# Sixteen-sequence attention and expert block on one core: the last sequence's output projections split into eight parts, its residual, norm and gates moved behind the first expert list

## The chip, the cores and the metric

The kernel runs on one core of a Trainium2 chip. The metric is the device time of one launch in microseconds (us), taken as the median of three runs. A core has a matrix engine (TensorE, PE in the tables), a vector engine (VectorE, DVE), an activation engine (ScalarE, ACT), a general engine (GpSimd, POOL) and a queue that issues transfers (SyncE, SP). Each engine runs its own instructions strictly in the order in which the kernel was built, and the engines wait for one another by semaphores.

## The reference

The input is x of 16 sequences, 256 tokens and 256 features. What matters here, cut from the reference:

```python
h = _ln(x, ln1_g, ln1_b) + shift
qkv = (h @ Wqkv.T).reshape(b, n, 3, H, HD)          # 16 heads of 64
...                                                 # norms of q and k, softmax attention
x = x + o @ Wout.T                                  # output projection and residual
tok = x.reshape(-1, d)                              # 4096 tokens
gate = jax.nn.softmax(tok @ Wgate.T, axis=-1)       # 8 experts
k_cap = bs // E                                     # 512
vals, idx = jax.lax.top_k(gate.T, k_cap)            # each expert takes its 512 best tokens
g = _ln(tok[idx_flat], mlp_g, mlp_b)
y = gelu(g @ fc1[e].T + b1) @ fc2[e].T + b2         # per expert, weighted by the gate
tok = tok.at[idx_flat].add(y.reshape(-1, d))
```

## The kernel before

**Attention.** Each of the 16 sequences is two tiles of 128 tokens. The steps of all sequences are laid into one list (`plan.step`, in the code `at`), and each step has a number in the table `PLACES`. The steps are emitted in the order of these numbers, so `PLACES` alone sets the order of instructions on every engine. The numbers are places and not times of the profile.

**The tail of a sequence** (class `Tail`, once for each of its two tiles): `project` (L936) is the output projection, eight matmuls with 256 columns each, which the profile counts as 16 because the data is float32; `residual` (L943, then the statistics L623 and L625) runs on DVE; `power` (L629, L106) on POOL; `apply` (L635) on DVE writes the normed tokens; `transposes` (L962) on PE, `evict` (L968) on ACT, `gate` (L973) on PE and `gate_evict` (L979) on DVE make the gate logits; `store` (L947) and `store_norm` (L957) go through SP.

**The search.** The first routing picks, for every expert, tokens out of the first 15 sequences (half of the capacity), so it needs nothing from the last one. It finds the threshold of each expert bit by bit, in 30 rounds. In a round DVE compares (`compare_less`, L1101), PE counts with one small matmul into `pc` (`count_over`, L1110), and DVE decides the bit (`decide`, L1125). A round cannot begin before the one ahead is decided. The last sequence's attention is spread between these rounds on the other engines. Behind the counts of the last 20 rounds stand four transposes of an identity matrix on PE (`fill`, L557), which compute nothing that is used.

**The lists.** After the search come masks, running sums and places (L1140 to L1183). Then each of 16 jobs (8 experts of the first routing, 8 of the second) gets its list: `onehot` (L1246) makes 30 tiles on DVE, `list_matmul` (L1254) puts them through PE into `pls`, `take` (L1263, L1265) reads the row numbers and weights, and `gather` (L1270) fetches the rows by two indirect DMAs that POOL issues. `transposes` (L1279) into `px` and `evict` (L1286) bring the rows into the layout for `up` (L1333), `gelu` and `down` (L1353). On PE the order around the first job is: list 0, fillers (`fill(16)` twice), 20 of the 30 matmuls of list 1, `px` of job 0, 5 more of list 1, `fill(8)`, the last 5, and then `up` of job 0. The second routing, which does need the last sequence, begins inside job 1.

**PSUM.** `ps` has three tags that matter: `mm` with 3 buffers, `sc` with 4 and `po` with one. The gate logits `pl` and the list sums `pls` share the single buffer of `po`.

Of the kernel before, what the change touches and what calls it, by code (L numbers as in the profile page):

```python
# [9 lines left out]
F32 = mybir.dt.float32  # L10
# [8 lines left out]
P = 128  # L19
B, N, D = 16, 256, 256  # L20
# [8 lines left out]
HP = H // 2  # L29
# [37 lines left out]
def kernel(  # L67
# [84 lines left out]
    def make_others():  # L152
# [352 lines left out]
        742.67, 743.91, 745.19, 752.11, 757.25, 758.03, 744.67, 746.15, 753.02, 754.08, 757.05,  # L505
        749.01, 758.75, 759.99, 745.47, 746.71, 747.5, 753.93, 763.49, 764.15, 747.31, 748.46,
        755.75, 756.81, 757.54, 749.78, 765.16, 747.51, 749.18, 752.52, 754.84, 755.9, 756.56,
        749.95, 751.07, 756.66, 764.69, 765.35, 753.76, 766.36, 767.6, 772.57, 776.44, 777.59,
        777.59, 778.45, 778.96, 779.57, 780.01, 780.87, 781.59, 776.07, 779.94, 781.09, 781.09,
        781.95, 782.46, 781.32, 781.76, 782.25, 782.93, 224.23, 226.04, 227.04, 228.04, 229.04,  # L510
        230.04, 731.12, 732.47, 733.9, 750.61, 745.77, 747.11, 747.91, 749.11, 749.55, 750.55,
        751.06, 751.82, 751.51, 752.17, 752.42, 753.17, 752.87, 753.52, 753.93, 754.52, 754.38,
        754.72, 754.97, 755.57, 755.42, 755.92, 756.17, 756.72, 756.62, 756.92, 757.18, 757.72,
        757.63, 757.93, 758.18, 758.72, 758.63, 758.93, 759.18, 759.77, 759.63, 760.12, 760.38,
        760.92, 760.83, 761.13, 761.38, 761.92, 761.83, 762.13, 762.38, 762.93, 762.83, 763.13,
        763.13, 763.59, 764.13, 763.39, 764.33, 764.33, 764.58, 765.13, 765.03, 765.33, 769.09,
        765.59, 766.18, 766.04, 766.53, 768.09, 766.78, 767.38, 767.23, 767.73, 767.73, 767.98,
        768.53, 768.43, 768.73, 768.73, 768.99, 769.53, 769.44, 769.74, 769.73, 769.99, 770.53,
        770.44, 770.74, 770.74, 770.99, 771.54, 771.44, 771.74, 771.74, 772, 772.54, 772.45,
        772.75, 780.15, 773, 776.04, 773.45, 776.24, 780.51, 777.44, 779.54, 777.89, 779.74,  # L520
        779.79, 780.94, 781.54, 781.39, 781.75, 781.74, 782.28, 782.83, 782.73, 783.09, 783.03,
        783.34, 783.89, 783.79, 784.09, 784.09, 784.35, 784.89, 784.8, 785.1, 785.09, 785.35,
        785.89, 785.8, 786.1, 786.1, 786.35, 786.9, 786.8, 787.1, 787.1, 787.36, 787.9, 787.81,
        788.11, 788.1, 788.36, 788.9, 788.81, 789.11, 789.1, 789.36, 790.58, 790.58, 792.03,
        793.25, 794.37, 790.9, 794.37, 806.29, 753.97, 751.5, 767.6, 795.32, 795.32, 796.32,
        796.94, 797.85, 795.32, 798.92, 796.13, 799.28, 798.56, 799.64, 797.75, 800, 800.36,
        800.78, 800.36, 802.18, 805.94, 805.28, 805.94, 800.78, 801.43, 803.78, 802.24, 804.14,
        803.05, 804.5, 803.86, 804.86, 804.67, 805.72, 805.48, 806.84, 809.23, 809.65, 814.15,
        814.84, 808.23, 809.55, 812.55, 815.55, 807.18, 808.27, 808.05, 809.14, 808.92, 810.01,
        811.53, 812.62, 810.66, 811.75, 813.27, 814.36, 809.79, 810.88, 812.4, 813.49, 807.43,  # L530
        814.94, 818.62, 818.4, 822.08, 819.22,
    )

    if True:
# [5 lines left out]
        ps = ctx.enter_context(tc.tile_pool(name="ps", bufs=1, space=PSUM))  # L540
# [387 lines left out]
        class Tail:  # L928
# [2 lines left out]

            def project(self, a=0, b=HP):
                if a == 0:
                    self.pw = ps.tile([P, D], F32, tag="mm", bufs=3, name="pw")
                for hp in range(a, b):
                    nc.tensor.matmul(  # L936
                        self.pw, oTs[self.b][:, hp // 2, self.t, hp % 2, :], wo[:, hp, :],
                        start=(hp == 0), stop=(hp == HP - 1),
                    )
# [260 lines left out]
        class Job:  # L1200
# [177 lines left out]
            mm=3, sc=4, po=1, xs=5, hT=2, qT=2, kT=2, v=2, oT=2, xn=4, sq=2, ss=4, qk=3, nmax=8,  # L1378
            sums=4, pr=PRB, pb=3, qraw=2, prT=4, blocks=4, tok=3, tn=2, tokT=2, pa=1, l1=4, l2=4,
        ))  # L1380
        at = plan.step
# [19 lines left out]
        for b in range(B):  # L1401
# [6 lines left out]
            a = First(b)  # L1408
# [9 lines left out]
            for (g, t), p in GROUP.items():  # L1418
                p += base
                a = Group(b, g, t)  # L1420
                n = (b, g, t)
# [27 lines left out]
            for d in range(HP // 2):  # L1449
                a = Quad(b, d)  # L1450
                p = base + d * QUAD
                g = d // 2
                n = (b, d)
                po = ("po", 0) + n
# [24 lines left out]
            for t in range(TB):  # L1479
                a = Tail(b, t)  # L1480
                p = base + TAIL[t]
                n = (b, t)
                pw, tok, tn, tokT, l2, pg, pl = ("mm", 4) + n, ("tok",) + n, ("tn",) + n, ("tokT",) + n, ("l2",) + n, ("mm", 5) + n, ("po", 1) + n
                at(p, "PE", 3.47, a.project, [("oT", b)], [pw], [pw, ("oT", b)], lag=0.22)
                at(p + 4, "DVE", 1.0, a.residual, [pw], [tok], [pw, ("xs", b), tok, l2], lag=0.15)
                at(p + 5, "SP", 0.5, a.store, [tok], (), [tok], lag=2.0)
                at(p + 5, "POOL", 0.76, a.power, [tok], [l2], [l2])
                at(p + 6, "DVE", 0.33, a.apply, [l2], [tn], [l2, tok, tn], lag=0.18)
                at(p + 7, "SP", 0.5, a.store_norm, [tn], [("xnd", b)], [tn], lag=2.0)
                at(p + 6, "PE", 0.22, a.transposes, [tok], [pg], [tok, pg], lag=0.22)  # L1490
                at(p + 7, "ACT", 0.3, a.evict, [pg], [tokT], [pg, tokT], lag=0.19)
                at(p + 8, "PE", 0.45, a.gate, [tokT], [pl], [tokT, pl], lag=0.22)
                at(p + 9, "DVE", 0.16, a.gate_evict, [pl], [("gates", b)], [pl])
# [21 lines left out]
        for n in range(29, -1, -1):  # L1515
            pc = ("mm", 99, 30 - n)
            at(top + 1.3 * (30 - n), "DVE", 0.45, partial(first.compare_less, n), [("cand", n + 1)], [("cnt", n)], lag=0.095)
            at(top + 1.3 * (30 - n) + 0.1, "PE", 0.03, partial(first.count_over, n), [("cnt", n)], [("pc", n)], [pc], lag=0.17)
            at(top + 1.3 * (30 - n) + 0.2, "DVE", 0.2, partial(first.either, n), [("cand", n + 1)], [("next", n)])
            at(top + 1.3 * (30 - n) + 0.3, "DVE", 0.2, partial(first.decide, n), [("pc", n), ("next", n)], [("cand", n)], [pc], lag=0.053)  # L1520
            if n < 20:
                at(top + 1.3 * (30 - n) + 0.2, "PE", 0.36, partial(fill, 4), [("pc", n)], (), [("sc", 98, n)], lag=0.22)
        p1, p2 = ("mm", 99, 31), ("mm", 99, 32)
        top += 50
# [13 lines left out]
        for n in range(2):  # L1538
            a = jobs[n]
# [5 lines left out]
            for i in range(6):  # L1545
                name, took, by = {"D": ("DVE", 0.81, nc.vector), "P": ("POOL", 1.4, nc.gpsimd), "A": ("ACT", 3.5, nc.scalar)}[who[i]]
# [54 lines left out]
        for k in range(1, len(jobs)):  # L1601
            a = jobs[k]
# [4 lines left out]
            for s in range(SLOTS):  # L1607
# [36 lines left out]
                else:  # L1644
                    i, q = divmod(s - FC, 4)
# [66 lines left out]
```

## Time and profile before

| what | value |
|---|---|
| median of three runs | 1072.86 us (1072.36 to 1073.65) |
| the profiled execution, own time | 1076.07 us |
| its span in the trace | 1074.4 us |
| mean granted TensorE clock | 0.987 |
| busy: PE, DVE, ACT, POOL | 1039.2, 825.8, 588.7, 615.8 us |
| first list's row numbers ready on DVE (L1263) | begins at 814.03 us |
| first `up` matmul (L1333) | begins at 821.19 us |

Times of the trace count from the start of the span. A busy share is the time in which at least one instruction of the engine ran. The granted clock is the share of full speed that TensorE was allowed in a stretch. "Idle before" and the arrow in square brackets name the time an engine stood still before an instruction and what ended it.

### The profile page before, as it was taken

The page shows a single profiled execution, that of the slowest core. Times are in us where ns is not written, and L with a number is a line of the kernel's source. Part 1 is how long each engine was busy: PE and PEld are TensorE (multiplying, and loading weights), DVE is VectorE, ACT ScalarE, POOL GpSimd, SP SyncE. Part 2 cuts the span into 40 slices and gives each one's busy share as a digit, 9 for nine tenths or more (in the row PEclk, how much of TensorE's full clock was granted, in tenths as well). Part 3 has the DMA queues.
Part 4 walks back from the last instruction along what each step waited for, and adds up shares of the span by engine and source line. Part 5 has one row for each costly group of instructions (what it writes and reads, how often), then busy time and mean ns, then how long its engine had stood idle before and what let it go on. Part 6 is the DMA issues. An engine that isn't in the chain of part 4 may idle for free. (4 is left out here: it accounts for less than half of the span.)

```text
span 1074.4 us, 17749 instructions
## 1 busy us (share of the span) xinstructions
PE 1039.2 (97%) x5519; PEld 680.7 (63%) x5519; DVE 825.8 (77%) x2295; ACT 588.7 (55%) x1646; POOL 615.8 (57%) x997
## 2 busy tenths in 40 slices
PE   7899999999999999999999999999789999999996
PEld 4455656555554655656565565666568888888885
DVE  6667888989887898798888888888667588656530
ACT  1577676676666666575766667675503422332331
POOL 3666776778667686666767676674401433333332
PEclk9999999999999999999999999999899999999998
DMA  6014889888887898887888888888530656667772
GB/s 217 1 59 157 270 292 325 291 291 280 305 275 264 284 317 309 289 287 271 286 295 301 285 299 286 289 314 288 176 103 21 195 143 182 197 199 202 219 233 30
DMA packets 169710, 250.53 MB, mean 233 GB/s; under 512 B 9744, under 2 KB 139536, under 8 KB 169616
## 3 DMA queue, kind: packets, MB, share of 16 engines
q1 hardware_dynamic: 161696, 239.11, 65.5%
q0 software_dynamic: 6144, 8.39, 4.3%
q10 hardware_dynamic: 1776, 1.90, 0.5%
q8 instruction: 44, 0.72, 0.3%
q14 instruction: 50, 0.41, 0.1%
HBM read 142.67 MB, written 106.69 MB: 232 GB/s over the span
## 5 line engine op out<-in xcount | busy, mean ns | idle before, releaser
L696 PE MATMUL pm<-wq,hT 128*128 128x512 f32 x768 | 360.8, 607 | 7.9 <-DVE qk L733 4.2
L843 ACT ACTIVATE pr<-sc,nmax 128x256 f32<-128x256 f32 x512 | 237.3, 479 | 102.4 <-DVE nmax L830 86.7
L854 POOL TENSOR_SCALAR pr<-pr,sums 128x256 f32<-128x256 f32 x512 | 237.0, 481 | 97.6 <-DVE sums L850 91.6
L696 PEld LDWEIGHTS pm<-wq,hT 128*128 128x128 f32 x768 | 137.8, 191 | 162.9 <-issue 136.2
L106 POOL TENSOR_TENSOR ss<-ss,neghalf 128x8 f32<-128x8 f32 x128 | 210.5, 1645 | 10.6
L830 DVE TENSOR_REDUCE nmax<-sc 128x2 f32<-128x512 f32 x256 | 165.7, 676 | 15.1 <-PE sc L822 14.4
L864 DVE STREAM_TRANSPOSE pb<-pr 128x512 f32<-128x512 f32 x232 | 153.9, 686 | 7.2 <-POOL pr L854 6.7
L822 PE MATMUL sc<-kT,qT 64*128 64x256 f32 x1024 | 135.2, 394 | 0.0
L910 PE MATMUL po<-prT,v 128*64 128x256 f32 x1024 | 128.8, 389 | 0.0
L709 ACT ACTIVATE sq<-pm 128x512 f32<-128x512 f32 x128 | 76.7, 604 | 92.4 <-PE pm L696 91.4
L1370 POOL DMA_INDIRECT out<-y,idx x32 | 50.9, 1591 | 124.7 <-DVE oh L1246 59.9
L822 PEld LDWEIGHTS sc<-kT,qT 64*128 64x128 f32 x1024 | 91.3, 186 | 46.9 <-issue 28.5
L1333 PE MATMUL ph<-xT,w 128*128 128x256 f32 x512 | 116.9, 383 | 2.2 <-ACT xT L1318 2.2
L936 PE MATMUL pw<-wo,oT 128*128 128x256 f32 x512 | 115.2, 381 | 0.0
L1353 PE MATMUL py<-w,hid 128*128 128x256 f32 x512 | 115.1, 380 | 0.0
L936 PEld LDWEIGHTS pw<-wo,oT 128*128 128x128 f32 x512 | 96.3, 190 | 21.0 <-issue 6.0
L910 PEld LDWEIGHTS po<-prT,v 128*64 128x64 f32 x1024 | 66.7, 137 | 65.3 <-issue 19.6
L843 ACT ACTIVATION_READ_ACCUMULATOR pr<-sc,nmax 128x1 f32 x512 | 108.0, 211 | 0.0
L733 DVE TENSOR_TENSOR qk<-pm,ss 128x512 f32<-128x512 f32 x128 | 89.7, 702 | 22.1 <-POOL ss L106 20.0
L1333 PEld LDWEIGHTS ph<-xT,w 128*128 128x128 f32 x512 | 95.0, 190 | 16.4 <-ACT xT L1318 3.5
L1353 PEld LDWEIGHTS py<-w,hid 128*128 128x128 f32 x512 | 96.1, 190 | 13.2
L713 DVE TENSOR_REDUCE ss<-sq 128x8 f32<-128x512 f32 x128 | 85.0, 669 | 22.8 <-ACT sq L709 21.3
(144 smaller groups left out, 1058.3 us busy)
## 6 DMA issues: line engine op xcount, KB each, us to landing
blocks<-pb SPq DMA_DIRECT2D x116, 512.0 KB
prT<-blocks SPq DMA_DIRECT2D x116, 512.0 KB
kblocks<-kb SPq DMA_DIRECT2D x60, 512.0 KB
w<-in_fc2T SPq DMA_DIRECT2D x16, 1024.0 KB
qraw<-kblocks SPq DMA_DIRECT2D x30, 512.0 KB
kT<-kblocks SPq DMA_DIRECT2D x30, 512.0 KB
w<-in_fc1T SPq DMA_DIRECT2D x9, 1024.0 KB
w<-in_fc1Q SPq DMA_DIRECT2D x7, 1024.0 KB
```

Source lines behind the costliest of these rows:

```text
L106: nc.gpsimd.tensor_tensor(dst, src, neghalf[:, : src.shape[1]], ALU.pow)
L696: nc.tensor.matmul(self.pm, hTs[self.b][:, c, bass.ts(self.t, P)], wq[:, c, bass.ts(self.g, GW)], start=(c == 0), stop=(c == DC - 1),)
L733: engine.tensor_tensor(dst, src.rearrange("p (q e d) -> p q e d", q=QB, e=8), by_head(self.ss[:, 1, :]), ALU.mult,)
L822: nc.tensor.matmul(self.sc[i, j][:, t, :], qTs[self.b][rows, hp, bass.ts(t, P)], keys[rows, hp] if whole else keys[rows, hp // 4, hp % 4], ...
L830: nc.vector.tensor_reduce(self.nmax[i, j], self.sc[i, j], AX.X, ALU.max, negate=True)
L843: nc.scalar.activation(dst, src, AF.Exp, bias=self.nmax[i, j][:, t : t + 1], scale=1.0, accum_out=self.sums[i][:, 0, j, t : t + 1],)
L854: nc.gpsimd.tensor_scalar(self.pr[i, j][:, t, :], self.pr[i, j][:, t, :], self.sums[i][:, 1, j, t : t + 1], 1.0, ALU.mult, ALU.mult,)
L864: nc.vector.transpose(self.pb[i][:, :, :, j].rearrange("p k c t n -> p t k c n"), self.pr[i, j].rearrange("p t (k c m) -> p t k c m", c=TB ...
L910: nc.tensor.matmul(self.po[j * HD : (j + 1) * HD, i, :], vs[self.b][:, c, bass.ts(4 * self.d + 2 * i + j, HD)], prT[:, j, c] if (self.b, s ...
L936: nc.tensor.matmul(self.pw, oTs[self.b][:, hp // 2, self.t, hp % 2, :], wo[:, hp, :], start=(hp == 0), stop=(hp == HP - 1),)
L1333: nc.tensor.matmul(self.ph[f], self.w1[:, c, bass.ts(f, P)], self.xT[:, :, c].rearrange("p k i n -> p k (i n)") if self.exchanged else sel ...
L1353: nc.tensor.matmul(self.py[i], self.hid[:, f, bass.ts(i, P)], self.w2[:, f, :], start=(f == 0), stop=(f == FC - 1),)
```

## The change

The two projections of the last sequence, which stood whole behind two counts of the search, are cut into four parts of two matmuls (four in the profile's count) each. One part stands behind each of eight counts, and the four filler transposes that stood behind these counts are left out. The target of these projections moves from the PSUM tag `mm` to `sc`. All that follows them (residual, power, apply, transposes, evict, gate, gate_evict, both stores) gets places behind `take` of the first list; the projections of the other 15 sequences are untouched. Seen on the engines: on DVE both residuals with their statistics stand between `take` of list 0 and `gives` of list 1, and both `apply` and both `gate_evict` between that and the 30 one-hot tiles of list 1; on POOL both `power` stand between the two gathers of job 0 and those of job 1; on PE the gate's transposes and matmuls stand between the two `fill(16)`; on SP the second job's weights are issued ahead of the four stores, as before.

```diff
     PLACES = (
...
-        749.95, 751.07, 756.66, 764.69, 765.35, 753.76, 766.36, 767.6, 772.57, 776.44, 777.59,
-        777.59, 778.45, 778.96, 779.57, 780.01, 780.87, 781.59, 776.07, 779.94, 781.09, 781.09,
-        781.95, 782.46, 781.32, 781.76, 782.25, 782.93, 224.23, 226.04, 227.04, 228.04, 229.04,
+        749.95, 751.07, 756.66, 764.69, 765.35, 753.76, 766.36, 767.6, 769.54, 770.54, 771.55,
+        772.55, 800.37, 800.83, 800.79, 800.82, 800.85, 800.82, 800.84, 800.89, 800.91, 776.05,
+        779.55, 781.55, 782.84, 800.38, 800.84, 800.8, 800.83, 800.86, 800.83, 800.85, 800.95,
+        800.97, 224.23, 226.04, 227.04, 228.04, 229.04, 230.04, 731.12, 732.47, 733.9, 750.61,
...
             def project(self, a=0, b=HP):
                 if a == 0:
-                    self.pw = ps.tile([P, D], F32, tag="mm", bufs=3, name="pw")
+                    tag, bufs = ("sc", 4) if self.b == B - 1 else ("mm", 3)
+                    self.pw = ps.tile([P, D], F32, tag=tag, bufs=bufs, name="pw")
...
-                at(p, "PE", 3.47, a.project, [("oT", b)], [pw], [pw, ("oT", b)], lag=0.22)
+                steps = 4 if b == B - 1 else 1
+                for i in range(steps):
+                    part = (i * HP // steps, (i + 1) * HP // steps)
+                    at(p, "PE", 3.47 / steps, (partial(a.project, *part) if steps > 1 else a.project), [("oT", b)] + ([(1, pw, i)] if i else []), [(1, pw, i + 1)] + ([pw] if i == steps - 1 else []), [pw, ("oT", b)], lag=0.22)
...
-            if n < 20:
+            if n < 20 and not 5 < n < 14:
                 at(top + 1.3 * (30 - n) + 0.2, "PE", 0.36, partial(fill, 4), [("pc", n)], (), [("sc", 98, n)], lag=0.22)
```

## The prediction

> **What bounds the kernel now.** I read the page first: PE is busy for 1039.2 of 1074.4 us, so what counts is whether PE's order stands still, and where. The timeline of PE through the search shows the rounds that the change touches:
>
> ```profile
> 785.25 0.16 PE L1110 MATMUL pc<-cnt,twice 128*128 128x1 bf16 x1 [0.34 <-DVE reach L1101]
> 785.28 0.64 PE L557 MATMUL fill<-ident 128*128 128x128 f32 x4
> 786.25 0.16 PE L1110 MATMUL pc<-cnt,twice 128*128 128x1 bf16 x1 [0.34 <-DVE reach L1101]
> ...
> 787.28 3.70 PE L936 MATMUL pw<-wo,oT 128*128 128x256 f32 x16
> 790.82 0.17 PE L1110 MATMUL pc<-cnt,twice 128*128 128x1 bf16 x1
> 790.84 3.70 PE L936 MATMUL pw<-wo,oT 128*128 128x256 f32 x16
> 794.38 0.17 PE L1110 MATMUL pc<-cnt,twice 128*128 128x1 bf16 x1
> ...
> 798.82 0.16 PE L1110 MATMUL pc<-cnt,twice 128*128 128x1 bf16 x1 [0.34 <-DVE reach L1101]
> ```
>
> A plain round lasts 1.00 us and waits for DVE's compare (PE idles 0.34). Where a whole projection stands between two counts, the count comes 3.54 us after the projection began and nothing is idle on PE: there PE holds the search. Next, the same view where the first list hands over to the first job (DVE, POOL and PE, one after the other):
>
> ```profile
> 814.03 0.16 DVE L1263 TENSOR_REDUCE idx<-pls 128x2 int32<-128x4 f32 x1 [0.40 <-PE pls L1254]
> 816.06 0.96 POOL L1270 DMA_INDIRECT xg<-xn_dram,idx  x1 [0.30 <-issue]
> 819.55 0.64 PE L1279 MATMUL px<-ident,xg 128*128 128x128 f32 x4
> 820.02 0.27 PE L1254 MATMUL pls<-give,oh 128*128 128x10 bf16 x5
> 820.15 1.07 PE L557 MATMUL fill<-ident 128*128 128x128 f32 x8
> 821.06 0.27 PE L1254 MATMUL pls<-give,oh 128*128 128x10 bf16 x5
> 821.19 7.15 PE L1333 MATMUL ph<-xT,w 128*128 128x256 f32 x32
> ```
>
> The first job starts behind the whole of list 1 in PE's order, so whatever makes DVE late with list 1's one-hot tiles makes the first `up` late. After 821.19 PE has no gap for the next jobs (in the stretches from 821 to 870 its busy time equals their length), so a shift of the first `up` carries over to the end. Last, the busy time cut into stretches of 3.41 us, with the granted clock in the third column from the end:
>
> ```profile
> 801.30:804.71 3.41, 2.18 (x17) 1.48 (x16) 2.91 (x18) 0.00 (x0) 0.00 (x0) 1.00 0.82 289
> 811.53:814.95 3.42, 3.04 (x35) 2.34 (x35) 2.98 (x19) 0.96 (x4) 0.45 (x1) 1.00 0.02 7
> 814.95:818.36 3.41, 3.41 (x18) 3.41 (x17) 3.41 (x23) 0.00 (x0) 1.77 (x2) 0.50 0.27 77
> ```
>
> The clock was halved at 814.95 and came back at 818.36, although PE counts as busy for 3.04 us of the stretch ahead. What differs is the work: list matmuls of 10 columns, with only about 1.1 us of transposes, against 2.18 us of fillers that kept it.
>
> **What is saved: the search.** From the count at 784.25 to the one at 798.82 are eight rounds in 14.57 us. A projection of 16 took 3.54, so a part of 4 takes 0.885 us; with the 0.03 from count to first matmul that is 0.92, under the 1.00 of the round that DVE sets (a round with eight filler transposes, about 0.97 from 783.28 to the next count, also held 1.00). DVE's residuals (1.01 each, from 791.19 to 792.20), `apply` and gate copies leave these rounds too. Eight rounds at 1.00 make 8.00: the search ends **6.57 us** earlier. The removed fillers cost nothing to take out, since the parts keep PE denser than they did. The move to the `sc` tag leaves two buffers for the fillers of rounds 5 to 0; one filler group per round needs no more. Job 1's weights wait for the last projection (SP's issue at 794.61) and now go out about 2 us earlier, into a quiet DMA stretch; the row gather comes later, so I count nothing.
>
> **What is given back: list 1.** I count from the start of the first list's row numbers (0 = 814.03 before), at full clock.
> - DVE: both residuals stand ahead of list 1's `gives`: 2 x 1.01, so `gives` moves from 0.15 to 2.17 and ends its slot at 2.69.
> - POOL: both `power` are queued behind the two gather issues, which end at 2.99. With the 0.30 that POOL showed after one such issue (the trace has no arithmetic behind one; between 0 and 0.30, I take 0.30, the only row) the first `power` ends at 4.11 (0.82, from 792.37 to 793.19), the second at 4.93. DVE's two `apply` wait for them, the second until about 4.97, and behind them wait the gate copies and all 30 one-hot tiles.
> - One buffer: the second gate matmul needs the `po` buffer that the first gate copy frees. Copy 5.29 to 5.46, matmul at 5.51, second copy 0.55 to 0.65 later (795.97 to 796.52, 797.27 to 797.92), first one-hot 0.10 after it, at 6.21. Before: 0.67 (814.70). **5.54 us later.**
> - PE: `px` waits for 20 one-hots and the last fillers for 25. The tiles come at 0.167 each (30 in 5.00), 25 by 10.38; from the five list matmuls at 820.02 to `up` were 1.17, of which 0.1 is the first of them, so `up` starts at about 11.5 instead of 7.16: **4.34 us** back.
>
> The rows themselves are no limit: those of job 0 were there by 819.55 (5.5), now `px` comes at 9.6. Those of job 1: its row numbers come 7.09 after its first one-hot (814.70 to 821.79), at 13.3; the DMA activity ended 3.8 after them (825.6), at 17.1; PE gets there 6.99 after `up` starts, at 18.5. The four stores wait on SP behind the new `apply`; behind them stands only job 2's load, which waits for job 0's `down` anyway. Second routing and later one-hots begin with job 1 and have 5.33 us of DVE idle ahead of them before (832.27).
>
> **The clock.** At full clock the sum is 6.57 - 4.34 = 2.23 us saved. But PE now waits in pieces: between list 0 and `up` it has 11.5 us, and in them two groups of 16 fillers (1.75 each), the gate's transposes (0.5), `px` (0.5) and eight fillers (0.9). From the end of the second group at 7.8 to `up` at 11.5 only 1.4 us of dense work lies in 3.7 us. The rows bracket the limit: 1.1 in 3.41 lost the clock, about 1.5 (three filler rounds, 0.5 each without pipeline end) kept it. If it is lost there, `px` and eight fillers take up to 1.4 more and the first 3.41 us of `up` do half their work, 1.7 more: 0 to 3.1; less than 0 is excluded, for the 2.23 has no half clock on its path. Between the ends I take 1.4, because 1.4 lies nearer to the row that kept the clock and the stretches need not fall on the worst place. The sum is **0.8 us saved**: 1076.07 becomes 1075.2 for the profiled execution, which ran 3.2 above the median (its clock and times are those of one run); the same step on the median gives 1072.0.
>
> [...]
>
> **The rivals.**
> 1. *No clock lost* (faster): 2.23 saved, up to 3.0 if POOL has no gap behind its issues and the waits are a little shorter: 1070.6 (1069.8 to 1070.7). For it: the 1.4 against 1.5 is close. Against it: the halved clock at 814.95 in the same kind of work.
> 2. *Half clock all along* (slower): the clock drops at list 0 as before, the thin stretch behind it (gate matmuls of 8 columns, waits) cannot bring it back, as 774.00 to 777.42 with 1.88 us busy stayed at 0.50, and it stays halved through `px`, the fillers and two stretches of `up`: 1.4 + 3.4 = 4.8 lost, 2.6 slower, 1075.4. It decides for the slower side from 2.23 + 2.15 = 4.4 us of loss on.
> 3. *A part does not fit in a round*: the round with attention matmuls from 781.12 to 782.24 took 1.12. Eight such rounds cost 1.0 of the gain: 1071.6 to 1073.0, with or without the clock; it stays in the middle case.
>
> **How the numbers follow.** A measurement of this kernel tells about 0.2% from no change, 2.15 us. The middle case (0.8 saved, between 2.15 saved and 2.15 lost) has 0.45, rival 1 has 0.30, rival 2 has 0.25. The middle case alone spans 1070.8 to 1075.0. The range 1069.8 to 1075.6 takes in the best of rival 1 and the price of rival 2, and leaves out what lies beyond either. The time is that of the middle case.
>
> **What would show it.** In the profile after: counts 1.00 apart with four `pw` matmuls between them from the count at 784.25 on; row numbers of list 0 near 807.5; then 5.5 us until list 1's first one-hot, with DVE's `apply` ended by POOL's `power`; `up` 11.5 behind the row numbers, near 819.0 at full clock and 820 to 821 with the loss; and a clock of 0.50 in a stretch between. Wrong would be: counts wider than 1.1 apart, a one-hot start much before 5 us, or a gap at job 1's `px`.

## The result, and the profile after

The changed kernel took 1071.01 us (median of 20 runs), the kernel before, measured beside it, 1073.37 (20 runs). The ratio is 0.9978, with a 95% interval of 0.9969 to 0.9987: **2.4 us saved, between 1.4 and 3.3**. The profiled execution took 1070.36 us (span 1068.6). Lines of the new kernel from L936 on are one higher than before.

PE's timeline through the search, with start, duration and, in brackets, the idle time ahead:

```profile
782.44 0.16 PE L1111 MATMUL pc<-cnt,twice 128*128 128x1 bf16 x1
782.47 1.11 PE L937 MATMUL pw<-wo,oT 128*128 128x256 f32 x4
783.44 0.16 PE L1111 MATMUL pc<-cnt,twice 128*128 128x1 bf16 x1
...
790.47 0.16 PE L1111 MATMUL pc<-cnt,twice 128*128 128x1 bf16 x1
```

The same eight rounds that took 14.57 us (784.25 to 798.82) now take 8.03 (782.44 to 790.47). The bracket is gone: PE waits for nothing ahead of a count, and the round is still 1.00. The hand-over from list 0 to the first job, in the timelines of DVE, POOL and PE:

```profile
805.74 0.16 DVE L1264 TENSOR_REDUCE idx<-pls 128x2 int32<-128x4 f32 x1 [0.42 <-PE pls L1255]
809.69 0.41 DVE L635 TENSOR_SCALAR tn<-tok,mv,rs 128x256 f32<-128x256 f32 x1 [1.17 <-POOL rs L106]
810.61 0.41 DVE L635 TENSOR_SCALAR tn<-tok,mv,rs 128x256 f32<-128x256 f32 x1 [0.50 <-POOL rs L106]
811.86 0.17 DVE L980 COPY gates<-pl 128x8 f32<-128x8 f32 x1 [0.77 <-PE pl L974]
811.94 4.97 DVE L1247 TENSOR_SCALAR oh<-lane,partf 128x128 bf16<-128x128 bf16 x30
807.77 0.96 POOL L1271 DMA_INDIRECT xg<-xn_dram,idx  x1 [0.31 <-issue]
808.80 0.19 POOL L629 TENSOR_SCALAR rs<-mv 128x1 f32<-128x1 f32 x1
811.24 0.58 PE L974 MATMUL pl<-wg,tokT 128*128 128x8 f32 x4 [0.95 <-DVE gates L980]
817.23 7.15 PE L1334 MATMUL ph<-xT,w 128*128 128x256 f32 x32
```

Both `apply` wait for POOL, the second gate matmul for the first gate copy (the one `po` buffer), the second copy for that matmul. List 1's first one-hot tile starts at 811.94, 6.20 us behind the row numbers, and `up` 11.49 behind them; before it was 0.67 and 7.16. Last, the busy time in stretches of 3.41 us (PE first, the granted clock third from the end):

```profile
805.22:808.63 3.41, 3.41 (x23) 3.35 (x23) 2.72 (x11) 0.00 (x0) 2.12 (x2) 0.50 0.23 55
808.63:812.04 3.41, 2.21 (x19) 1.91 (x18) 1.08 (x5) 0.65 (x2) 1.61 (x5) 1.00 0.45 151
812.04:815.45 3.41, 3.41 (x36) 3.35 (x35) 3.41 (x22) 0.00 (x0) 0.00 (x0) 0.50 0.07 24
815.45:818.86 3.41, 3.41 (x33) 3.14 (x31) 3.31 (x16) 1.49 (x3) 0.00 (x0) 1.00 0.03 7
```

The clock drops twice: over the first 16 fillers (0.50 from 805.22), where it dropped in the kernel before too (0.50 from 814.95), and again between the lists (0.50 from 812.04), as the prediction feared. But the 16 fillers of the second group fill that second slow stretch, and `up` begins 1.78 us after full speed is back. In this run the second drop cost nothing.

### One table for all runs

Medians of the kernel before went from 1071.85 to 1073.28 us over four chips, so the traces are read by four intervals on one path. *Search*: from the count behind which the first part stands (784.25 before, the same count in all) to the first matmul of the totals (804.84 before). *List 0*: to the first list's row numbers. *List 1*: to the first `up`. *Job 0*: to the `up` of job 1 (835.53 before). Sum is their change against 51.28; time is ratio minus one, times the median of before on the same chip, with the interval.

| run | search | list 0 | list 1 | job 0 | sum | time, us |
|---|---|---|---|---|---|---|
| before | 20.59 | 9.19 | 7.16 | 14.34 | | |
| before, second trace | 20.58 | 9.19 | 7.16 | 14.33 | 0.0 | +0.1 (-1.4 to 1.5) |
| after | 14.02 | 9.28 | 11.49 | 14.33 | -2.2 | -2.4 (-3.3 to -1.4) |
| after, second trace | 14.02 | 9.26 | 12.64 | 14.83 | -0.5 | -1.8 (-3.3 to -0.2) |
| parts only, tail in the search | 17.33 | 9.19 | 7.15 | 14.34 | -3.3 | -2.9 (-4.1 to -1.8) |
| tail moved only, no parts | 19.53 | 9.93 | 12.35 | 14.33 | +4.9 | +4.6 (3.2 to 6.0) |
| gates behind list 1 | 14.02 | 9.27 | 7.92 | 15.62 | -4.5 | -4.4 (-6.0 to -2.7) |
| whole tail behind list 1 | 14.02 | 9.26 | 7.16 | 16.32 | -4.5 | -4.2 (-5.6 to -2.8) |
| `power` ahead of the gathers | 14.02 | 9.26 | 10.78 | 14.34 | -2.9 | -1.5 (-3.0 to 0.0) |
| no fillers | 14.02 | 9.28 | 11.83 | 16.73 | +0.6 | +0.6 (-0.9 to 2.1) |
| eight more fillers | 14.02 | 9.28 | 11.50 | 14.34 | -2.1 | -1.0 (-2.5 to 0.5) |
| spread, first order | 14.02 | 9.26 | 9.10 | 14.34 | -4.6 | -5.8 (-7.7 to -3.9) |
| spread, second order | 14.02 | 9.35 | 8.89 | 14.33 | -4.7 | -5.0 (-7.0 to -3.1) |
| spread, eight fillers fewer | 14.02 | 9.35 | 8.84 | 14.79 | -4.3 | -5.5 (-7.2 to -3.6) |

### The profile page after: what moved, and what is told of

It is laid out like the page before. It is cut to its first block, busy times and chain, and to the rows that moved or that the text cites. A ratio compares the mean times of both kernels' runs of the same rounds, so it can differ in the third digit from the quotient of the medians.

```text
span 1068.6 us, 17684 instructions
## 1 busy us (share of the span) xinstructions
PE 1036.7 (97%) x5487; PEld 678.7 (64%) x5487; DVE 826.2 (77%) x2295; ACT 588.3 (55%) x1646; POOL 616.1 (58%) x997
## 4 chain that ended last, share of the span: by engine, by line
PE 87%; DVE 5%; DMA 4%; POOL 2%; issue 1%; ACT 1%; POOLq 0%; SPq 0%; DVEq 0%; ACTq 0%
PE pm L696 31%; PE sc L822 11%; PE po L910 11%; PE pw L937 10%; PE ph L1334 9%; PE py L1354 9%; DMA wq<-in_wqkvT 1%; DMA xg<-xn_dram,idx 1%; PE pl L974 1%; PE pp L891 1%; PE pls L1255 1%; DVE oh L1247 1%; PE fill L557 1%; PE pg L963 1%; DVE nmax L830 1%
```

## The experiments

The edits are mostly new places for the steps of the last sequence's tail (two numbers: first and second tile).

**The parts alone.** The rest of the tail goes back into the search.

```diff
-residual 800.37, 800.38   apply 800.82, 800.83   transposes 800.82, 800.83
-gate 800.89, 800.95       gate_evict 800.91, 800.97
+residual 776.25, 784.095  apply 779.75, 785.11   transposes 779.56, 784.9
+gate 781.56, 785.9        gate_evict 782.74, 786.81
```

> The changed kernel with its eight projection parts, but with the residuals, `apply`, gate matmuls and gate copies of the last sequence back inside the search, one piece to a round. Theory (PE's whole projections held the search; the late list 1 gave back 4.3 us): the search saves 6.5 us and takes up to 3.2 again (2 x (1.01 + 0.41 + 0.17) of DVE in its rounds, less the 0.34 that DVE waits for PE in each), so it is 3.3 to 4.5 us shorter than before; list 1's first one-hot is 0.7 behind the first row numbers and `up` 7.2; total 3.3 to 4.5 us faster than before, 1 to 2 us faster than the changed kernel. Rival (the gain comes from taking the tail out of the search, not from the parts): counts return to 14 us for eight rounds and the time is that of before or slower.

The search took 17.33 us, and list 1 came as before; 2.9 us faster than before (trace: 3.3). The tail's pieces, DVE's above all, cost 3.3 us in the search. At most 0.4 of that is the clock: it was at half speed from 797.3 to 800.7, over three rounds of 1.31, 1.08 and 1.03 us. PE's timeline shows the round with the first residual, 1.86 us long:

```profile
787.88 0.16 PE L1111 MATMUL pc<-cnt,twice 128*128 128x1 bf16 x1
787.91 1.11 PE L937 MATMUL pw<-wo,oT 128*128 128x256 f32 x4
789.74 0.16 PE L1111 MATMUL pc<-cnt,twice 128*128 128x1 bf16 x1 [0.72 <-DVE reach L1102]
```

So the parts give the gain, and the move behind list 0 is not needed for it: set against this run, the changed kernel's first trace saves 3.3 us in the search and loses 4.4 later.

**The move alone.** Starting from the kernel before (projections whole, on the `sc` tag), the tail gets the places of the changed kernel.

```diff
-residual 776.44, 779.94   power 777.59, 781.09   apply 778.45, 781.95
-gate 780.87, 782.25       gate_evict 781.59, 782.93
+residual 800.37, 800.38   power 800.79, 800.80   apply 800.82, 800.83
+gate 800.89, 800.95       gate_evict 800.91, 800.97
```

> The kernel before with its two projections whole, each behind one count, and only the residuals, `apply`, gate matmuls and gate copies moved behind the first list. Theory: eight rounds go from 14.6 to 13.1 us (two rounds of 3.54 and six of 1.00), 1.45 saved; `up` comes 11.5 instead of 7.2 us behind the first row numbers, 4.3 given back; 2.9 us slower than before. Rival (what the tail costs behind list 0 is hidden, or the tail was what lengthened the search): within 1 us of before, or faster.

It was 4.6 us slower, and the table says where the sum was short: the search gained 1.06 (1.45 expected), list 0 lost 0.74 and list 1 5.19 (4.3 expected). The search's missing 0.39 us is nearly all one round of 1.37, in which twelve fillers stand between two counts. The other two are mostly the clock, at half speed in this trace in two places:

```profile
796.30:799.71 3.41, 2.16 (x19) 1.56 (x19) 2.95 (x16) 0.00 (x0) 0.00 (x0) 1.00 0.43 159
800.00:803.41 3.41, 3.41 (x19) 3.20 (x18) 1.67 (x6) 0.00 (x0) 0.00 (x0) 0.54 0.00 0
803.41:806.82 3.41, 2.62 (x23) 2.08 (x22) 3.34 (x16) 2.39 (x8) 0.89 (x2) 1.00 0.00 0
810.23:813.64 3.41, 3.27 (x15) 2.78 (x13) 1.98 (x7) 0.75 (x2) 2.77 (x6) 0.50 0.51 154
813.64:817.05 3.41, 2.43 (x12) 2.46 (x13) 1.89 (x12) 0.00 (x0) 0.31 (x1) 0.50 0.24 82
```

In the first of them (800.00 to 803.41) the places' eight transposes took 2.00 instead of 1.33 us, 0.67 of the 0.74. In the last two rows the gate matmuls took 1.0 each instead of 0.6, and the first one-hot came 6.61 instead of 6.20 behind the row numbers, half of what list 1 lost beyond the changed kernel's 4.33. The top row is the stretch ahead of the first drop. It holds three filler groups behind counts, as the kernel before had from 801.30 to 804.71 (2.18 us busy) and kept full speed after.

**Only the residuals ahead of list 1.**

```diff
-power 800.79, 800.8   apply 800.82, 800.83   transposes 800.82, 800.83
-gate 800.89, 800.95   gate_evict 800.91, 800.97
+power 806.5, 806.51   apply 812.56, 812.57   transposes 809.8, 809.81
+gate 811.6, 813.4     gate_evict 812.58, 815.56
```

> The changed kernel with only the residuals left ahead of list 1; `power`, `apply`, the gate matmuls and gate copies go behind list 1's one-hot tiles. Theory (DVE's order decides when `up` starts): first one-hot 2.7 us behind the first row numbers (two residuals), `up` at 8.0, 3.5 us faster than the changed kernel, 5.7 faster than before. Rival 1 (the clock decides): `up` at 8.0 but at half clock for its first 3.4 us, only 1.8 faster than the changed kernel. Rival 2 (POOL's queue or the row gather decides): `up` stays at 10 or later.

`up` came 7.92 us behind the row numbers, 0.1 from the theory. DVE's order sets it: the last one-hot tile ended at 814.34. But the whole gain was 4.4 us, not 5.7, and PE's timeline of the first job, below DVE's tiles, shows why:

```profile
809.38 4.96 DVE L1247 TENSOR_SCALAR oh<-lane,partf 128x128 bf16<-128x128 bf16 x30
814.66 3.70 PE L1334 MATMUL ph<-xT,w 128*128 128x256 f32 x16
818.20 0.60 PE L963 MATMUL pg<-ident,tok 128*128 128x128 f32 x4
818.64 1.89 PE L1334 MATMUL ph<-xT,w 128*128 128x256 f32 x8
820.37 0.51 PE L974 MATMUL pl<-wg,tokT 128*128 128x8 f32 x4
820.73 1.97 PE L1334 MATMUL ph<-xT,w 128*128 128x256 f32 x8
822.54 0.51 PE L974 MATMUL pl<-wg,tokT 128*128 128x8 f32 x4
```

Transposes and gate matmuls now stand where PE has no gap: job 0 is 1.28 us longer. Neither theory had counted that.

**The whole tail behind list 1.**

```diff
-residual 800.37, 800.38   transposes 800.82, 800.83   gate 800.89, 800.95
+residual 809.3, 809.31    transposes 812.41, 812.42   gate 814.93, 818.3
```

> The changed kernel with the whole tail of the last sequence, residuals too, behind list 1 and inside the first job. Theory: search 6.5 us shorter, list 1's first one-hot 0.7 and `up` 7.2 us behind the first row numbers as before; nothing is given back; 6.5 us faster than before, 4.3 faster than the changed kernel. Rival 1: the two projections keep two of the four PSUM buffers of the first matmuls of `up`, which then wait for the GELU: up to 1 us lost. Rival 2: the later gates delay the second routing and the loss returns at a later job.

List 1 is back at 7.16, so nothing is given back there. Again job 0 pays, 1.98 us: the same PE work and, among the rest, 0.39 us in which PE waits for ACT's copy `tokT`:

```profile
821.43 0.61 PE L974 MATMUL pl<-wg,tokT 128*128 128x8 f32 x4 [0.39 <-ACT tokT L969]
```

The 32 `up` matmuls are not held by missing buffers: 28 of them run unbroken in 6.29 us. It was 4.2 us faster than before; 6.5 was expected.

**POOL's order.**

```diff
-power 800.79, 800.8
+power 800.771, 800.772
```

> The changed kernel with both `power` put on POOL ahead of the first list's two gather issues. The prediction's term: behind the issues the two `power` hold `apply`, the gate copies and list 1's one-hot tiles. Theory (POOL's queue sets the end of the tail): `apply` starts about 2.7 us behind the row numbers, right behind `gives`, the two gate copies then set the first one-hot at about 5.2 instead of 6.2, the gather issues go out 1.7 later, the rows come at 7.2 to 7.5, which is still ahead of the 20th one-hot at 8.5; `up` at 10.5, 0.7 to 1.0 us faster than the changed kernel. Rival 1 (PE's transposes and gate matmuls hold the tail on their own): first one-hot stays at 5.9 to 6.2, no gain. Rival 2 (the rows come too late): `px` waits for them, `up` at 11.5 or later.

The first one-hot came 5.50 behind the row numbers instead of 6.20, `up` at 10.78 instead of 11.49. POOL's queue was worth 0.7 us, and what is late next is PE: the first 16 fillers, mostly at half clock, held PE until 808.73, so the gate matmuls came late:

```profile
805.81 3.12 PE L557 MATMUL fill<-ident 128*128 128x128 f32 x16
810.47 0.17 DVE L980 COPY gates<-pl 128x8 f32<-128x8 f32 x1 [0.87 <-PE pl L974]
```

The time, 1.5 us faster than before with an interval of 3, can't tell 0.7 from nothing; the trace can.

**No fillers.** The 16 + 16 + 8 transposes ahead of `up` are left out; nothing uses them.

```diff
-partial(fill, 16) (twice), partial(fill, 8)
+partial(fill, 1), which issues none
```

> The changed kernel without the 16 + 16 + 8 filler transposes between the first list and `up`. Theory (clock is granted by dense work; the fillers hold it): PE has only about 2 us of dense work in the 11 us ahead of `up`, the clock is halved when `up` starts and stays so for 1.4 to 4.8 us, so 0.7 to 2.4 us slower than the changed kernel, less up to 0.5 because the last eight fillers no longer stand ahead of the last list matmuls: 0.2 to 2.4 slower. Rival (the clock plays no part in this stretch): `up` starts up to 0.5 us earlier and the time is the same or up to 0.5 us better.

The clock was halved at 804.5 and stayed so to 821.5. Three stretches out of that time:

```profile
807.88:811.29 3.41, 0.90 (x4) 0.93 (x4) 0.90 (x3) 0.00 (x0) 1.52 (x4) 0.50 0.46 157
814.70:818.11 3.41, 3.41 (x20) 2.77 (x20) 3.34 (x17) 1.02 (x2) 0.00 (x0) 0.50 0.01 2
818.11:821.52 3.41, 3.41 (x9) 2.70 (x8) 3.38 (x23) 0.95 (x2) 1.96 (x2) 0.50 0.16 43
```

```profile
816.70 9.55 PE L1334 MATMUL ph<-xT,w 128*128 128x256 f32 x32
```

`up` took 9.55 us instead of 7.15; with `up` 0.34 later that is 2.7 us lost against the first trace of the changed kernel, and the whole gain is gone (+0.6 us, -0.9 to 2.1). So the clock plays its part here: its price is 2.4 us when `up` starts at half speed, and with the fillers `up` ran at full speed in the first trace of the changed kernel (7.15 us from 817.23, full speed from 815.45).

**Eight more fillers** behind the first gate matmul.

```diff
             def gate(self):
...
+                if self.b == B - 1 and self.t == 0:
+                    fill(8)
```

> The changed kernel with eight more filler transposes behind the first gate matmul, where PE waits 0.95 us for DVE's copy. The prediction counted 1.4 us for a clock lost between the first list and `up`. If that loss is there in a usual run: 0.5 to 1.4 us faster than the changed kernel. If it is not, as the traced run suggests (`up` ran at full clock and came 11.5 us behind the row numbers): within 0.4 us of it, or 0.9 us slower where the eight run at half clock and hold the second gate matmul.

The second filler group ran at full speed (1.94 us instead of 3.32), and `up` still came 11.50 behind the row numbers:

```profile
813.54 1.94 PE L557 MATMUL fill<-ident 128*128 128x128 f32 x16
815.32 2.07 PE L1257 MATMUL pls<-give,oh 128*128 128x10 bf16 x20
```

In this one trace the warmer clock bought nothing, because DVE's tiles were the limit there. On the time, 1.0 us faster than before (-2.5 to 0.5), it stays open.

**The pieces spread over waits that exist.** DVE waits 1.03 us for the places' transposes ahead of list 0; one residual goes there, the rest as the text says.

```diff
-residual 800.37, 800.38   transposes 800.82, 800.83   gate 800.89, 800.95   gate_evict 800.91, 800.97
+residual 793.3, 800.37    transposes 794.3, 800.82    gate 800.6, 802.19     gate_evict 801.5, 803.06
```

> The changed kernel with one residual moved into DVE's 1.03 us wait for the places' transposes, the other left behind the first list, the gate matmuls left in PE's wait ahead of `up` (one transposed pair ahead of list 0), the two gate copies between list 1's one-hot tiles, and `power`, `apply` and the stores behind them. Theory (each engine's piece goes where that engine waits anyway): eight rounds at 1.00, first one-hot of list 1 1.7 us behind the first row numbers, `up` 7.2 to 7.4, and no gate matmul inside the first job, which cost 1.3 to 2.0 us there: 6.3 to 6.5 us faster than before at full clock. Rival 1: the first residual does not fit in the wait and delays list 0 by up to 1 us. Rival 2: the clock, with less dense work in a row, is halved in `up`: 1.7 us less gain.

The residual is free there: list 0 took 9.26. No gate matmul stands in job 0 (14.34). But `up` came 9.10 behind the row numbers, because the first gate matmul is queued behind 16 fillers at half clock (3.56 us), and DVE waits for it between list 1's tiles, in its timeline:

```profile
809.20 0.17 DVE L980 COPY gates<-pl 128x8 f32<-128x8 f32 x1 [1.23 <-PE pl L974]
811.56 0.17 DVE L980 COPY gates<-pl 128x8 f32<-128x8 f32 x1 [0.57 <-PE pl L974]
```

**The same in a second order.**

```diff
-gate 800.6, 802.19   gate_evict 801.5, 803.06   partial(fill, 16), partial(fill, 16)
+gate 794.36, 800.6   gate_evict 796.0, 803.06   partial(fill, 8), partial(fill, 16)
```

> As the version with the pieces spread over the waits, but with the first gate matmul and its copy inside list 0, ahead of the 16 fillers there, and eight instead of 16 fillers ahead of the second sequence tile's transposes and gate matmul behind list 0. In the version before this one the first gate matmul stood behind 16 fillers at half clock and DVE waited 1.23 + 0.57 us for it in the middle of list 1. Theory: these waits go, list 0 is 0.1 longer, `up` comes 7.2 to 7.6 us behind the row numbers instead of 9.1; 6.0 to 6.4 us faster than before, 1.5 to 1.8 better than the version before. Rival (PE waits for ACT's copy ahead of list 0 and the fillers there run late, list 0 ends 0.5 to 1 us later or the clock drops in `up`): no better than the version before.

DVE's waits went, as expected, but `up` came only 0.2 us earlier. The fillers themselves took their place; PE's timeline:

```profile
804.87 1.95 PE L557 MATMUL fill<-ident 128*128 128x128 f32 x8
808.59 3.38 PE L557 MATMUL fill<-ident 128*128 128x128 f32 x16
811.80 0.65 PE L1255 MATMUL pls<-give,oh 128*128 128x10 bf16 x20
```

The 20 list matmuls had their tiles about 1.7 us earlier (the tiles start at 806.71, 0.167 each) and stood behind fillers at half clock.

**Eight fillers fewer.**

```diff
-partial(fill, 8), partial(fill, 16)
+partial(fill, 8), partial(fill, 8)
```

> As the version before this one, with eight instead of 16 fillers in the second group behind list 0 (8 + 8 in all). There `up` came 8.9 us behind the row numbers because the 8 + 16 fillers ran at half clock (1.95 and 3.38 us) and held list 1's first 20 list matmuls 1.4 us past their one-hot tiles. Theory: those 20 now start as the 20th tile comes, 5.1 us behind the row numbers, `up` at 7.3 to 7.6 if the clock is full there; 6.0 to 6.5 us faster than before. Rival (the fillers that are gone are missed: the clock is halved in the last fillers and in `up`): `up` at 8 to 8.5, its 32 matmuls 1 to 2 us longer, and 3.5 to 5 us faster than before.

The rival came true in its mechanism: the list matmuls started 5.27 us behind the row numbers, as wanted, but the clock stayed at half from 804.2 to 814.4, the last eight fillers took 1.95 instead of 1.07 us, and `up` started at 8.84 and lost 0.45 in job 0. Fewer fillers gained 0.05 us ahead of `up` and lost it again behind.

The three spread versions and the two with the gates behind list 1 gain 4.3 to 4.7 us by their traces, 2.1 to 2.5 more than the first trace of the changed kernel, and their intervals overlap. The first and the last spread version (1067.17 and 1068.1 us) lie clear of the changed kernel's interval, each against the kernel before on its own chip; none reached the 6 us and more that were expected of the spreading.

**Both kernels again.**

> The changed kernel itself once more, beside the version below. It gives a second profiled execution of it. Theory (full-clock sum 2.2 us, no clock term in a usual run): 1.2 to 3.4 us faster than before, `up` 11.4 to 11.6 us behind the first row numbers and at full clock. If the prediction's clock term is there in many runs: 0.8 us faster or less, and a stretch of 0.50 inside `up`.

> The kernel before once more, for a second profiled execution of it. The first shows the clock back at full speed 2.8 us ahead of `up`. If its clock is as much a matter of the run as that of the changed kernel, the interval from the count that the first part stands behind to `up` differs from 36.9 us by up to 1.6 us and fillers of 16 take 1.9 in one place and 3.4 in another; if it is fixed, the interval is 36.9 within 0.1. The time is that of before.

On this path the kernel before repeats to 0.02 us, although half speed began 0.94 us behind the row numbers in its first trace and 0.05 in its second. Elsewhere it doesn't repeat: the two spans are 1074.4 and 1070.6 us, 2.72 of the difference ahead of the path and 1.06 behind it. The changed kernel differs on the path itself. Its second trace has the same search and the same list 0, and then the clock:

```profile
808.78:812.19 3.41, 2.39 (x20) 2.09 (x19) 1.60 (x8) 0.65 (x2) 1.25 (x3) 1.00 0.39 129
812.19:815.60 3.41, 3.41 (x33) 3.16 (x32) 3.41 (x22) 0.00 (x0) 0.00 (x0) 0.50 0.02 5
815.60:819.01 3.41, 3.41 (x24) 3.11 (x23) 3.31 (x17) 1.02 (x2) 0.00 (x0) 0.50 0.01 2
```

```profile
811.31 2.84 PE L557 MATMUL fill<-ident 128*128 128x128 f32 x16
816.09 1.95 PE L557 MATMUL fill<-ident 128*128 128x128 f32 x8
818.01 7.64 PE L1334 MATMUL ph<-xT,w 128*128 128x256 f32 x32
```

Half speed lasted two stretches instead of one, through `px`, the last fillers and the first microsecond of `up`: 1.15 us ahead of `up` and 0.50 in it. What differs ahead of 815 is that the second filler group began 0.88 us before the stretch did (811.31 against 812.19), so part of it ran at full speed and it ended near 814.1; in the first trace it began 0.36 us before its stretch (811.68 against 812.04) and ended near 815.0. By this reading half a microsecond of fillers in the slow stretch decided how the clock went on in these two traces. Two other traces fit it: about 2.4 us of fillers and transposes in a slow stretch (spread, second order, 804.72 to 808.13) left the clock at half, about 2.9 (tail moved only, 816.78 to 820.19) brought it back. These sums are estimates from PE's timelines, and the reading is argued, not tried by itself.

Of the two expectations for this run, the trace shows the second (0.50 inside `up`), and the time, 1.8 us with an interval of 0.2 to 3.3, doesn't decide between them.

## Why the prediction was right or wrong

The forecast was 0.8 us saved, 1072.0 us; 2.4 were saved, 1071.0 us. The time came nearer than the saving, by luck: over 20 runs the kernel before took 0.5 us more than the median that the forecast started from. The saving lies just beyond the 2.15 that the prediction drew between its middle case and rival 1, and its interval takes in both. Step by step:

- **The search, 6.57 us**: right, 6.57 in the interval to the totals. A part of four fits in the round, and rival 3 falls: counts are 1.00 apart.
- **List 1, 4.34 us**: right, 4.33 (11.49 against 11.5 forecast). Two details inside it missed and cancelled: POOL's arithmetic starts 0.07 us behind a gather issue, not 0.30, and the second gate matmul starts 0.15 us after the copy that frees its buffer, not 0.05. The list of waits (`apply` on POOL, gate copies on PE) was as written, and moving `power` showed that the first of them carries 0.7 us.
- **List 0**: 0.09 us longer, not foreseen, and its cause stays open.
- **The clock, 1.4 us taken from 0 to 3.1**: this is the term that was mis-sized. The mechanism is real, half speed between the lists was there in both traces (0.50 from 812.04 to 815.45 and from 812.19 to 819.01), and it cost 0 in one and 1.6 in the other. Over runs it seems to cost less than 1.4: the full-clock sum is 2.2, the 20 runs saved at least 1.4 by their interval, so on average the clock took at most 0.8, if the two kernels are alike off this path. The reasoning weighed dense work against a limit but left out that the second filler group, slowed down, fills the slow stretch by itself while DVE is still making tiles. It had taken that group at its full-speed length, 1.75; it took 3.32 and was hidden. The limit itself is weaker than it was drawn: in the run with the tail moved only, a stretch with the same three filler groups as the row said to keep the clock (796.30 to 799.71) lost it. And the 2.18 us given as fillers in that row are all of PE's work there, counts included.
- **Rival 1** (no clock lost, 2.23 to 3.0 saved, 1070.6) describes what the first trace lost, though the clock did drop in it. **Rival 2** (half clock all along) did not happen with the fillers; without them it did, and cost 2.7 us.
- **Nothing behind**: right as far as the traces can tell. `px` of job 1 followed `up` without a gap (824.22), the stores did not show, and from the `up` of job 1 to that of job 8 all fourteen traces agree to 0.1 us (110.02 in the first trace of before, 110.06 in that of the changed kernel). Behind that single intervals between jobs scatter by up to 2 us over the runs (up to 0.55 between the two traces of the kernel before), and the cause stays open.

The drops did not follow PE's longest waits. In the kernel before, the longest wait of PE around list 0, 0.80 us (810.61 to 811.41), lies in a stretch that full speed followed (1.00 from 811.53); in the next stretch, from 811.53, no wait is longer than 0.27, 0.38 us in all, and half speed followed (0.50 from 814.95). Without the fillers the longest wait of PE was 2.57 us, and the clock stayed at 0.50 for 17 us.

## What to carry to other kernels

When a long step is cut to fit in the waits of a serial loop, ask of everything that hangs on it (its evictions, its norms, its own small matmuls) where each engine really waits: here the parts alone gave 3.3 us, and the tail moved to the front of the next serial stage gave 4.4 of the 6.6 back. A step taken off one engine's path can land on another's: DVE's tail behind list 1 was free on DVE and cost PE 1.3 to 2.0 us. Size fillers by what waits behind them at half speed, since that is the speed at which they may run: 16 of them took 3.3 to 3.6 us at half speed here, and 1.9 at full.

## What the runs showed of the hardware

- In these traces the granted clock changed at times that lie whole multiples of 3.41 us apart: 805.22, 808.63, 812.04 and 815.45 in the changed kernel's first trace, 805.37, 808.78, 812.19 and 819.01 in its second, 814.95 and 818.36 in the kernel before. Against the work these times lay differently from run to run: two runs of the changed kernel, half a microsecond apart in this, differed by 1.6 us in their path to the second job; two of the kernel before, 0.9 us apart, by 0.02.
- At half speed, stretches with about 2.4 us (804.72 to 808.13, spread, second order) and 2.5 us of fillers and transposes (812.19 to 815.60 of the changed kernel's second trace: fillers to about 814.1 and `px` from 815.02) did not bring full speed back; about 2.9 us did (812.04 to 815.45 of its first trace, fillers to about 815.0; 816.78 to 820.19 with the tail moved only).
- What keeps full speed is not bracketed. Three filler groups behind counts kept it in the kernel before (801.30 to 804.71, PE busy for 2.18 us) and lost it with the tail moved only (796.30 to 799.71, 2.16 us).
- PE's busy column doesn't tell what the clock will do. Without fillers, PE counts as busy for 3.41 us in the half-speed stretch 814.70 to 818.11, and the next is at half speed too; it counts as busy for 3.41 us in 818.11 to 821.52, and full speed follows.
